# Edge-gated graph layer: load and rows steps of groups 2 and 3, and the lists of blocks 4 to 7 in shorter pieces

## The chip, the cores and the metric

The kernel runs on one core of one Trainium2 chip. Its time is the device time of one execution in microseconds. The kernel before was timed in nine runs: median 1203.03 us, lowest 1196.97, highest 1206.84.

## The reference

There are 16 batches of 1024 nodes with 256 features, and one adjacency matrix of 1024 x 1024 in which few entries are not zero (the diagonal and about 0.8% of the rest). Every edge (u, v) of every batch has a gate, a sigmoid of a small network on the two nodes. Gated and ungated sums over the edges go through one weight matrix each and are added to the input:

```python
pre_u = jnp.einsum('bud,dk->buk', h_t, W1[:d])
pre_v = jnp.einsum('bvd,dk->bvk', h_t, W1[d:])
hidden = jax.nn.relu(pre_u[:, :, None, :] + pre_v[:, None, :, :] + b1)
S = jax.nn.sigmoid(jnp.einsum('buvk,ko->buvo', hidden, W2)[..., 0] + b2[0])
a_t = jnp.einsum('buv,bud->bvd', S * A_a, h_t)
m_t = jnp.einsum('uv,bud->bvd', A_m, h_t) * h_t
z_t = beta1 * h_t + beta2 * (a_t @ Wa + ba) + beta3 * (m_t @ Wm + bm)
```

The last line is shortened here; both products there are einsums. `A_a` and `A_m` are the same matrix.

## The kernel before, in words

The 16 batches are four groups of four (g = 0 to 3). The 1024 target nodes v are eight tiles of 128 (vt = 0 to 7). A block is one (g, vt): 32 blocks, in the order of line 365: the first six tiles of groups 0 and 1, then tiles 6 and 7 of both, then groups 2 and 3. A block has ten steps, two windows of 64 target nodes with five slots of 128 edges each. Step n is block n // 10 and place s = n % 10, and there are 320 steps.

**Edges instead of the full matrix.** `lists(vt)` (line 236) finds the edges of a tile. It loads a tile of the adjacency matrix (`key`), finds the largest keys of every row (`max`), spreads them over slots, and leaves index tables: `uidx` (which node row to fetch), `vidx` (which matrix entry), `onehot`, `whose` and `rest` (what did not fit). It is a generator: each `yield` ends a piece, and each `next(made[vt])` runs one. Nearly all of its work is on DVE; the matmuls into `pw` and `pe` are small, and for vt >= 3 they use the PSUM buffers "misc", of which there are two and which `rows`, `halves`, `turn_over` and `block_end` use too. The lists of tiles 0 to 3 are made ahead of step 0. Those of tiles 4 to 7 are made inside the steps, where `advance` (line 659) says which step runs a piece.

**Tables.** A group's table holds, for every node, its product with the first half of W1 and its input, so that one gather fetches both. `load_hT(k)` loads a transposed tile of the input on SP's queue, and waits until one of the ten buffers "hT" is free. `copy_h(k)` copies the input tile into the table, from memory to memory, on ACT's queue. `rows(k)` makes the product in two pieces, each with eight matmuls for `w_u` (line 384) and a copy on ACT (line 400), and stores it one step after the second (line 403, SP's queue). For the tiles that are not made ahead of step 0, `plan` (line 665) gives a triple: the step of the load, and the steps of the two pieces. The four blocks in `again` have their hT loaded a second time.

**A step.** `expand(n + 2)` puts the target nodes' products into PSUM `pc` with two matmuls (line 523). `gate(n)` adds the fetched rows (DVE, line 539), takes the weighted sum of the positive part for four batches (DVE, line 543), then ACT takes the sigmoid (line 546) and scales the left factors (line 549). `aggregate(n - 1)` sums on PE with 8 or 16 matmuls (line 560). `fetch(n + 4)` gathers 128 table rows into one of five buffers "fetched" on POOL (line 453); it needs aggregate(n - 1) to have left that buffer, and the gathers of a group need its whole table. `fetch_val(2)` (line 341) issues up to two small gathers of matrix entries on POOL in each step, as long as any list has left some.

**Once a block.** `halves(k + 1)` multiplies the next block's hT by `w_v` at places 0 and 2 (line 384 again), and ACT copies at places 3, 5 and 6. `turn_over` transposes sums at places 1, 7 (twice) and 9. `block_end` multiplies by Wm and Wa at places 3 to 6. The output is stored at place 9 (line 615), and the input block is loaded at place 0 (line 714), both on SP's queue. A hT buffer becomes free when `times_h` (line 591, DVE) has read it, at place 3 of the block after the one that used it.

**Order.** The order of instructions on each engine and queue is written by hand: the loop of line 684 goes through the steps, and each engine works through its own in that order, waiting on semaphores only. SP has little but transfers, so it runs ahead of the steps until a transfer has to wait for data or for a buffer. What `after(step, f)` registers runs at `do(n)`, after gate(n). At step 100, POOL reduces `rest` over the partitions (line 761).

Of the kernel before, what the change touches and what calls it, by code (L numbers as in the profile page):

```python
# [11 lines left out]
ALU = mybir.AluOpType  # L12
AX = mybir.AxisListType
P = 128
# [3 lines left out]
def kernel(  # L18
# [42 lines left out]
    nc = tc.nc  # L61
    B, N, D = x.shape
    NT = N // P
# [41 lines left out]
    def fixed(shape, name, dt=FP):  # L105
        return const.tile(shape, dt, name=name)
# [5 lines left out]
    ukey = fixed([P, N], "ukey")  # L112
# [117 lines left out]
    EARLY = 4  # L230
# [3 lines left out]


    def lists(vt):
        key = fetched[vt + 1][:, :N] if vt < EARLY else big.tile([P, N], FP, name="key", bufs=1)
        (nc.sync if 2 <= vt < EARLY else nc.gpsimd).dma_start(key, adjT[vt * P:(vt + 1) * P, :])
        yield
# [1 line left out]
        top = R[:, 5:5 + S]  # L241
        count = wk.tile([P, 1], FP, name="count", bufs=4)
        unread = one.tile([P, N], mybir.dt.uint8, name="unread")
        nc.vector.scalar_tensor_tensor(key, key, 0.0, ukey, ALU.not_equal, ALU.mult)
        nc.scalar.activation(unread, key, AF.Sign, accum_out=count)
        yield

# [1 line left out]
        cand = wk.tile([P, N // P, 8], FP, name="cand", bufs=2)  # L249
        for c in range(N // P):  # L250
            nc.vector.max(cand[:, c, :], key[:, c * P:(c + 1) * P])
        yield
        cut = wk.tile([P, 1], FP, name="cut", bufs=2)
        nc.vector.tensor_reduce(cut, cand[:, :, 7], AX.X, ALU.max)
# [2 lines left out]
        for s in range(0, S, 8):  # L257
            nc.vector.max(top[:, s:s + 8], keys)
            if s + 8 < S:
                nc.vector.scalar_tensor_tensor(keys, keys, top[:, s + 7:s + 8], keys, ALU.is_lt, ALU.mult)  # L260

        used = wk.tile([P, S], FP, name="used", bufs=4)
        nc.vector.tensor_scalar(used, top, 0.0, None, ALU.is_gt, ALU.add, accum_out=R[:, 0:1])
# [29 lines left out]
        last = wk.tile([P, 1], FP, name="last", bufs=4)  # L293
        nc.vector.scalar_tensor_tensor(used, nth, held, top, ALU.is_equal, ALU.mult, accum_out=last)
        nc.vector.tensor_tensor(thr[:, vt:vt + 1], last, none, ALU.add)
        RR = wk.tile([P, NW, RC], FP, name="RR", bufs=2)
        few = wk.tile([P, E], mybir.dt.uint8, name="few", bufs=2)
        nc.scalar.copy(few, mark)  # L298
        for w, mine in enumerate((soon, late)):
            nc.vector.tensor_scalar(RR[:, w, :], R, mine, None, ALU.mult)  # L300
        yield
# [4 lines left out]
        for j in range(TW):  # L306
            nc.tensor.matmul(pe[:, j * NW * RC:(j + 1) * NW * RC], mark[:, j * P:(j + 1) * P],
                             RR.rearrange("p w r -> p (w r)"), start=True, stop=True)
        M = NW * TW
# [6 lines left out]
        eq = wk.tile([P, M, S], FP, name="eq", bufs=1)  # L316
        nc.vector.tensor_tensor(eq, nth.unsqueeze(1).to_broadcast([P, M, S]),
                                s_of.unsqueeze(2).to_broadcast([P, M, S]), ALU.is_equal)
        nc.vector.tensor_tensor(eq, eq, L[:, :, 5:], ALU.mult)
        k_of = wk.tile([P, M], FP, name="k_of", bufs=2)  # L320
        nc.vector.tensor_reduce(k_of, eq, AX.X, ALU.add)
        sl = slice(vt * NW, (vt + 1) * NW)
        nc.vector.tensor_scalar(uidx[:, sl].rearrange("p w j -> p (w j)"), k_of, -1.0, float(N), ALU.mult, ALU.add)
        nc.vector.tensor_tensor(k_of, L[:, :, 2], k_of, ALU.subtract)
# [132 lines left out]


    made = [lists(vt) for vt in range(NT)]
    turn = [(g, vt) for g in range(2) for vt in (*range(FIRST, NT), *range(FIRST))]  # L460
    tabs = [fetched[0][:, :GD], *(f[:, GD:] for f in fetched)]
# [195 lines left out]


    advance = {0: (3,), 2: (3,), 4: (3,)}
    for i, n in zip(range(EARLY, NT), (0, 20, 50, 80)):  # L660
        for o in (0, 4, 5, 6, 7, 9, 11, 13, 15, 17):
            advance[n + o] = (*advance.get(n + o, ()), i)
    loads, at = {}, {}

    def plan(blocks, ns):

        for k, (load, *pieces) in zip(blocks, ns):
            loads[load] = k
            at.update((n, k) for n in pieces)

    plan(turn[NT:], ((0, 5, 8), (6, 12, 15), (12, 18, 22), (17, 25, 28), (24, 32, 35), (31, 38, 42), (38, 45, 48),
                     (43, 50, 52)))
    plan([(2, vt) for vt in range(NT)], ((62 + 10 * i, 68 + 10 * i, 73 + 10 * i) for i in range(NT)))
    plan([(3, vt) for vt in range(NT)], ((146, 152, 157), (156, 162, 167), *((153 + 10 * i, 158 + 10 * i, 161 + 10 * i)
                                                                             for i in range(2, NT))))
    plan(again, ((103,), (113,), (125,), (133,)))
    begun = set(turn[:NT])
    end = parts = piece = last = None
# [5 lines left out]
    for n in range(total + 2):  # L684
        k, s = divmod(n, T)
# [25 lines left out]
        if s == 0 and 0 < k < BS:  # L711
            hbs[k - 1] = big.tile([P, GB, D], FP, name="h_blk", bufs=1)
            g, vt = order[k - 1]
# [56 lines left out]
    with tc.If(any_left > 0):  # L770
        with ExitStack() as s2:
# [3 lines left out]
            for vt in range(NT):  # L775
# [12 lines left out]
                key = fb.tile([P, N], FP, name="fb_key")  # L788
# [88 lines left out]
```

## Time and profile before

| | us |
|---|---|
| median of nine runs | 1203.03 |
| the profiled execution | 1199.47 |
| its span | 1197.7 |
| start of step 0 (first L539) | 74.0 |
| start of step 100 | 464.6 |
| start of step 160 | 665.2 |
| start of step 240 | 929.0 |

| engine | busy us | share of the span |
|---|---|---|
| PE, matmuls | 1101.6 | 92% |
| DVE | 1064.6 | 89% |
| ACT | 896.9 | 75% |
| POOL | 433.8 | 36% |

The DMA engines move 391 MB, 327 GB/s over the span. The busy time of PE is modelled where matmuls are pipelined, so 92% is no measure of how much it could still do. A step is found in the trace by its L539, the first DVE instruction of gate(n), of which there are 320. Times in the trace count from the start of the span.

### The profile page before, as it was taken

The page shows a single profiled execution, that of the slowest core. Times are in us where ns is not written, and L with a number is a line of the kernel's source. Part 1 is how long each engine was busy: PE and PEld are TensorE (multiplying, and loading weights), DVE is VectorE, ACT ScalarE, POOL GpSimd, SP SyncE. Part 2 cuts the span into 40 slices and gives each one's busy share as a digit, 9 for nine tenths or more (in the row PEclk, how much of TensorE's full clock was granted, in tenths as well). Part 3 has the DMA queues.
Part 4 walks back from the last instruction along what each step waited for, and adds up shares of the span by engine and source line. Part 5 has one row for each costly group of instructions (what it writes and reads, how often), then busy time and mean ns, then how long its engine had stood idle before and what let it go on. Part 6 is the DMA issues. An engine that isn't in the chain of part 4 may idle for free. (4 is left out here: it accounts for less than half of the span.)

```text
span 1197.7 us, 23914 instructions
## 1 busy us (share of the span) xinstructions
PE 1101.6 (92%) x7633; PEld 726.8 (61%) x7633; DVE 1064.6 (89%) x3483; ACT 896.9 (75%) x2624; POOL 433.8 (36%) x428
## 2 busy tenths in 40 slices
PE   6856899989899989999999999999999999999986
PEld 5743566656556656666666566666666666666653
DVE  7688879978998897999999889989999999999994
ACT  2346577768768867888888788888888888888873
POOL 1556762533253326333333233233323333333330
PEclk9878998989899999999999999999999999999999
DMA  9986898999988989999999999999999999999992
GB/s 280 284 281 232 263 342 319 347 327 339 336 281 301 380 281 312 368 376 378 384 349 359 336 338 361 347 367 367 361 359 361 348 323 331 322 337 329 333 348 84
DMA packets 147047, 391.40 MB, mean 327 GB/s; under 512 B 16752, under 2 KB 105328, under 8 KB 110704
## 3 DMA queue, kind: packets, MB, share of 16 engines
q0 software_dynamic: 50016, 300.50, 68.4%
q1 hardware_dynamic: 81616, 74.99, 19.7%
q10 hardware_dynamic: 15280, 14.29, 3.7%
q8 instruction: 63, 1.03, 0.3%
q14 instruction: 72, 0.59, 0.1%
HBM read 393.78 MB, written 50.33 MB: 371 GB/s over the span
## 5 line engine op out<-in xcount | busy, mean ns | idle before, releaser
L453 POOL DMA_INDIRECT fetched<-table,uidx x320 | 336.2, 1051 | 669.2 <-PE acc L560 514.5
L543 DVE SCALAR_TENSOR_TENSOR t<-t,w_b 128x256 f32<-128x256 f32 x1280 | 469.5, 422 | 22.0
L539 DVE TENSOR_TENSOR t<-fetched,pc 128x1024 f32<-128x1024 f32 x320 | 389.5, 1217 | 68.1 <-DMA fetched<-table,uidx 29.4
L560 PE MATMUL acc<-fetched,left 128*32 128x256 f32 x4096 | 342.0, 393 | 35.2 <-ACT left L549 29.3
L549 ACT ACTIVATE left<-left,gt 128x32 f32<-128x32 f32 (+1 forms) x1280 | 299.3, 304 | 10.4
L523 PE MATMUL pc<-X,mark 128*128 128x512 f32 x640 | 237.0, 452 | 12.3 <-DVE t L539 6.9
L560 PEld LDWEIGHTS acc<-fetched,left 128*32 128x32 f32 x4096 | 132.5, 110 | 185.6 <-ACT left L549 57.7
L523 PEld LDWEIGHTS pc<-X,mark 128*128 128x128 f32 x640 | 96.8, 190 | 147.2 <-issue 80.6
L546 ACT ACTIVATE gt<-sc,b_b 128x4 f32<-128x4 f32 x320 | 96.0, 300 | 56.1 <-DVE t L543 51.3
L384 PE MATMUL misc<-w_u,hT 128*128 128x256 f32 x448 | 110.9, 395 | 10.3 <-ACT few L298 3.6
L609 PE MATMUL misc<-w_m,LT 128*128 128x256 f32 x496 | 117.1, 379 | 0.0
L609 PE MATMUL misc<-w_a,LT 128*128 128x256 f32 x496 | 117.1, 379 | 0.0
L533 ACT ACTIVATE left<-onehot,val 128x128 f32<-128x128 bf16 (+1 forms) x320 | 116.5, 364 | 0.0
L384 PE MATMUL misc<-w_v,hT 128*128 128x256 f32 x448 | 106.6, 381 | 0.0
L543 DVE DVE_READ_ACCUMULATOR t<-t,w_b 128x1 f32 x1280 | 104.2, 81 | 0.0
L609 PEld LDWEIGHTS misc<-w_m,LT 128*128 128x128 f32 x496 | 94.0, 189 | 15.1
L609 PEld LDWEIGHTS misc<-w_a,LT 128*128 128x128 f32 x496 | 93.9, 189 | 14.9
L384 PEld LDWEIGHTS misc<-w_u,hT 128*128 128x128 f32 x448 | 87.1, 198 | 25.5 <-ACT few L298 3.7
L341 POOL DMA_INDIRECT val<-in_adjT_dram,vidx x80 | 84.7, 1059 | 31.3 <-issue 21.6
L384 PEld LDWEIGHTS misc<-w_v,hT 128*128 128x128 f32 x448 | 85.6, 191 | 13.9
L581 ACT COPY LT<-misc 128x512 f32<-128x512 f32 x128 | 70.9, 574 | 28.8 <-PE pc L523 10.2
L568 ACT COPY ev<-acc 128x512 f32<-128x512 f32 x128 | 75.5, 590 | 18.6 <-remote 7.1
(160 smaller groups left out, 898.7 us busy)
## 6 DMA issues: line engine op xcount, KB each, us to landing
h_blk<-in_x_dram SPq DMA_DIRECT2D x31, 512.0 KB
out_dram<-z SPq DMA_DIRECT2D x31, 512.0 KB
hT<-in_xT_dram SPq DMA_DIRECT2D x28, 512.0 KB
table<-tab SPq DMA_DIRECT2D x26, 512.0 KB
table<-in_x_dram ACTq DMA_DIRECT2D x24, 512.0 KB
fetched<-table,uidx POOLq DMA_INDIRECT x320
table<-in_x_dram SPq DMA_DIRECT2D x8, 512.0 KB
table<-fetched SPq DMA_DIRECT2D x6, 512.0 KB
```

The lines of the kernel that those rows point to most:

```text
L341: nc.gpsimd.indirect_dma_start(out=val[:, i, j:j + 1], out_offset=None, in_=adj_flat, in_offset=bass.IndirectOffsetOnAxis(ap=vidx[:, i, j: ...
L384: nc.tensor.matmul(p[:, bb * D:(bb + 1) * D], hT[:, 2 * h + bb, i, :], wt[:, i, :], start=(i == 0 and not begun), stop=(i == DC - 1), skip ...
L453: nc.gpsimd.indirect_dma_start(out=fetched[n % NF], out_offset=None, in_=table[g], in_offset=bass.IndirectOffsetOnAxis(ap=uidx[:, vt * NW ...
L523: nc.tensor.matmul(pcs[n][:, c], marks[n // TW][:, j * P:(j + 1) * P], cuts[k][:, w, c], start=True, stop=True)
L533: nc.scalar.activation(lefts[n][:, :m, :, 0, :], onehot[:, i, o:o + m, :].unsqueeze(2).to_broadcast([P, m, GB, V]), AF.Copy, scale=val[:, ...
L539: nc.vector.tensor_tensor(t, fetched[n % NF][:, :GD].rearrange("p (b d) -> p b d", b=GB), pcs.pop(n).rearrange("p (b d) -> p b d", b=GB), ...
L543: nc.vector.scalar_tensor_tensor(t[:, b, :], t[:, b, :], 0.0, w2_b, ALU.max, ALU.mult, accum_out=sc[:, b:b + 1])
L546: nc.scalar.activation(gt, sc, AF.Sigmoid, bias=b2_b)
L549: nc.scalar.activation(lefts[n][:, :m, b, 1, :], lefts[n][:, :m, b, 0, :], AF.Copy, scale=gt[:, b:b + 1])
L560: nc.tensor.matmul(accs[h][b * 2 * V:(b + 1) * 2 * V, r, :], left[:, i, b].rearrange("p k v -> p (k v)"), f[:, GD + b * D:GD + (b + 1) * D ...
L568: nc.scalar.copy(evs[q], accs.pop(q))
L609: nc.tensor.matmul(pz[:, bb * D:(bb + 1) * D], LTs[k][:, c, 2 * h + bb, i, :], wt[:, c, :], start=False, stop=(i == 0 and c == DC - 1), sk ...
```

## The change

Two things are changed. In `lists`, for tiles 4 to 7 alone (`fine`), six more yields are put in, and the first multiplication is done in two halves; `advance` runs a piece at offset 0 and then one in every step from offset 4 on, from the start steps 0, 19, 48 and 88 instead of 0, 20, 50 and 80. A list has 16 pieces, so the call at offset 19 finds nothing left.

In the plan for groups 2 and 3 other steps are given. Group 2: loads at 60 + 10i (before 62 + 10i), pieces at 68 + 10i and 71 + 10i (before 68 + 10i and 73 + 10i). Group 3: the loads of tiles 0 and 1 at 141 and 149 (before 146 and 156), those of tiles 2 to 7 at 153 + 10i as before; pieces of tiles 0 and 1 at 149, 151 and 158, 161 (before 152, 157 and 162, 167), of tiles 2 to 6 at 161 + 10i and 168 + 10i (before 158 + 10i and 161 + 10i), and of tile 7 at 231 and 234 (before 228 and 231).

```diff
     def lists(vt):
+        fine = vt >= EARLY
         key = fetched[vt + 1][:, :N] if vt < EARLY else big.tile([P, N], FP, name="key", bufs=1)
...
-        nc.vector.scalar_tensor_tensor(key, key, 0.0, ukey, ALU.not_equal, ALU.mult)
+        if fine:
+            nc.vector.scalar_tensor_tensor(key[:, :N // 2], key[:, :N // 2], 0.0, ukey[:, :N // 2],
+                                           ALU.not_equal, ALU.mult)
+            yield
+        rest_ = slice(N // 2 if fine else 0, N)
+        nc.vector.scalar_tensor_tensor(key[:, rest_], key[:, rest_], 0.0, ukey[:, rest_], ALU.not_equal, ALU.mult)
         nc.scalar.activation(unread, key, AF.Sign, accum_out=count)
         yield
...
             nc.vector.max(cand[:, c, :], key[:, c * P:(c + 1) * P])
+            if fine and c == N // P // 2 - 1:
+                yield
...
                 nc.vector.scalar_tensor_tensor(keys, keys, top[:, s + 7:s + 8], keys, ALU.is_lt, ALU.mult)
+            if fine and s == 8:
+                yield
...
         nc.vector.tensor_tensor(thr[:, vt:vt + 1], last, none, ALU.add)
+        if fine:
+            yield
...
                                 s_of.unsqueeze(2).to_broadcast([P, M, S]), ALU.is_equal)
+        if fine:
+            yield
         nc.vector.tensor_tensor(eq, eq, L[:, :, 5:], ALU.mult)
         k_of = wk.tile([P, M], FP, name="k_of", bufs=2)
         nc.vector.tensor_reduce(k_of, eq, AX.X, ALU.add)
+        if fine:
+            yield
...
-    for i, n in zip(range(EARLY, NT), (0, 20, 50, 80)):
-        for o in (0, 4, 5, 6, 7, 9, 11, 13, 15, 17):
+    for i, n in zip(range(EARLY, NT), (0, 19, 48, 88)):
+        for o in (0, *range(4, 20)):
             advance[n + o] = (*advance.get(n + o, ()), i)
...
-    plan([(2, vt) for vt in range(NT)], ((62 + 10 * i, 68 + 10 * i, 73 + 10 * i) for i in range(NT)))
-    plan([(3, vt) for vt in range(NT)], ((146, 152, 157), (156, 162, 167), *((153 + 10 * i, 158 + 10 * i, 161 + 10 * i)
-                                                                             for i in range(2, NT))))
+    plan([(2, vt) for vt in range(NT)], ((60 + 10 * i, 68 + 10 * i, 71 + 10 * i) for i in range(NT)))
+    plan([(3, vt) for vt in range(NT)], ((141, 149, 151), (149, 158, 161), *((153 + 10 * i, 161 + 10 * i, 168 + 10 * i)
+                                                                             for i in range(2, NT - 1)), (223, 231, 234)))
```

## The prediction, made before the changed kernel was seen

> **What bounds the kernel now.** I read the page first, then the windows view with an edge at the first L539 of every tenth step (a step is one gate(n); ten steps are one block), then the waits, then the timeline wherever a block was longer than its neighbours.
>
> The windows view, one row a block:
>
> ```profile
> core 0: us, PE busy (x) PEld busy (x) DVE busy (x) ACT busy (x) POOL busy (x), PEclk, DMA share, GB/s
> 388.30:428.80 40.50, 36.93 (x264) 24.01 (x262) 36.35 (x126) 30.63 (x91) 11.24 (x12) 0.96 0.95 344
> 428.80:464.60 35.80, 33.90 (x238) 22.73 (x242) 34.61 (x116) 27.58 (x81) 15.60 (x15) 1.00 0.84 291
> 464.60:501.20 36.60, 34.93 (x244) 22.90 (x236) 30.19 (x95) 27.89 (x83) 15.90 (x17) 1.00 1.01 361
> 501.20:534.10 32.90, 32.71 (x240) 21.65 (x232) 30.44 (x99) 27.81 (x82) 10.15 (x10) 1.00 1.02 376
> 632.10:665.20 33.10, 31.69 (x219) 20.79 (x216) 30.29 (x97) 26.52 (x77) 9.78 (x10) 1.00 0.97 352
> 665.20:700.90 35.70, 33.09 (x232) 21.58 (x232) 30.27 (x96) 27.52 (x83) 10.09 (x11) 1.00 0.89 325
> 700.90:734.30 33.40, 33.13 (x242) 21.36 (x243) 30.25 (x95) 28.09 (x87) 11.83 (x12) 1.00 1.00 361
> 734.30:765.60 31.30, 29.56 (x210) 19.47 (x209) 30.15 (x97) 26.24 (x79) 10.18 (x10) 1.00 0.99 357
> 929.00:960.30 31.30, 30.15 (x218) 19.22 (x217) 30.15 (x96) 26.33 (x80) 10.53 (x11) 1.00 0.96 350
> ```
>
> These are blocks 8 to 11, 15 to 18 and 24. Block 24 has only gates and aggregates: 31.3 us, of which DVE works 30.2. That is the floor, and block after block from 24 to 30 takes it. Block 18 has two pieces of rows as well and still takes 31.3. Blocks 8 and 9 share the list of block 7, which adds (36.35 + 34.61) - 2 x 30.2 = 10.6 us of DVE work; there DVE is the bound. In block 11 the DMA share is 1.02 and PE is busy nearly throughout. Blocks 15, 16 and 17 have no list, and stand 1.8, 4.4 and 2.1 us above the floor.
>
> The waits, and the timeline at the worst place of block 16:
>
> ```profile
> POOL fetched L453 <- PE acc L560: 514.5, 229, 6.9
> ...
> DVE t L539 <- DMA fetched<-table,uidx: 29.4, 27, 3.7
> ```
>
> ```profile
> 674.50 1.22 DVE L539 TENSOR_TENSOR t<-fetched,pc 128x1024 f32<-128x1024 f32 x1 [3.69 <-DMA fetched<-table,uidx]
> ...
> 676.58 1.89 PE L384 MATMUL misc<-w_v,hT 128*128 128x256 f32 x8
> ...
> 678.30 1.89 PE L384 MATMUL misc<-w_u,hT 128*128 128x256 f32 x8
> ...
> 681.49 0.99 POOL L453 DMA_INDIRECT fetched<-table,uidx  x1 [5.55 <-PE acc L560]
> ```
>
> The reader is to see a ring: PE aggregates, that frees a fetched buffer, POOL issues the gather, DVE gates, ACT makes left, PE aggregates. A late PE makes the next gather late, and a gather that is late is what DVE waits for. In block 16 the products for w_v (halves) and w_u (rows, step 162) fall on one step, and just before it three 512 KB transfers leave SP together: the timeline has table<-tab at 664.13, out at 664.57, h_blk at 665.34.
>
> **What the Trainium skill says.** "Perfetto Trace Analysis", Optimization Strategy: the most-contended engine can change between regimes, and interleaving regimes can help. The trace agrees: DVE bounds the list blocks (DMA 0.84 in block 9), DMA and PE the next ones. "DMA: Bandwidth & Descriptors", Issuing engines are not separate DMA queues: transfers of SP, ACT and POOL run on the same 16 engines. The trace agrees with shares of 1.00 to 1.02, so moving a transfer moves a delay. "TensorE: Matmul & The Clock Gate", Part 1, says that an idle PE falls to half clock; the page's PEclk has digits of 7 and 8 in early slices, and I price nothing by it.
>
> **The change, part by part.** The profiled execution took 1199.47 us (span 1197.7), the median of the nine runs is 1203.03; I sum against the former and move the median by the same amount.
>
> 1. Rows at the start of group 3. Pieces move from steps 152, 157, 162, 167, 178 to 149, 151, 158, 161, and one goes to the end (234). From i = 2 on, the other pieces keep the same steps (181, 188, ... 231) with another half in each. A piece is 8 matmuls, 1.89 us by the timeline row. Block 16 loses one of its two pieces and the collision at its third step, block 17 loses its only one, and block 15's go to its second and ninth steps, where PE has only an aggregate, an expand and at most a transpose. Before, the three blocks take 33.1 + 35.7 + 33.4 = 102.2 us. Blocks 20 to 23, with pieces at just these places, take 31.7, 32.5, 32.9 and 32.0 in the same view, a mean excess of 1.0 over the floor. With 3 x 32.3 = 96.9 the gain is 5.3 us. At most it is 102.2 - 93.9 = 8.3; at least 0, if DMA and not PE holds these blocks. I take 5.3.
>
> 2. Rows of group 2. The second pieces go from the fourth step of a block (73 + 10i) to its second (71 + 10i). The fourth already has 16 aggregating matmuls and the first products of block_end. In block 7 this ends a wait of 2.01 us at L539 of step 76 for PE pc; I count 1.0 back, and 0.3 in block 14. Blocks 6, 8, 9 are held by DVE, blocks 10 to 13 by DMA (shares 1.00 to 1.02): nothing there. The loads go from 62 + 10i to 60 + 10i. On SP this moves nothing: SP runs ahead, and hT (L373) already leaves about 0.6 us after h_blk (349.69, then 350.28), so "two steps earlier" is true of copy_h on ACT's queue only. Its 512 KB take about 512/370 = 1.4 us of the DMA engines, now beside out, h_blk and hT. In list blocks DVE hides it. In blocks 10 to 13 gathers for the fourth step are late already (up to 2.98 us), but PE is busy through those waits; bounds 0 to 4 x 1.4, taken 1.3. The table store comes two steps earlier, far from its first gather. Sum of the part 0.0.
>
> 3. The lists. The work on DVE stays: one multiplication of 1.22 us becomes two of half, some 0.1 us each list more, 0.4 in all. Within steps 24 to 39, 54 to 69 and 84 to 99 DVE idles no more than in the clean blocks, so an even spread gains nothing there. List 7 moves: its pieces run in steps 92 to 106, not 84 to 97. In block 10 the same view has DVE at 30.19 of 36.60 us, so 5.3 us of stall (floor idle taken off) in which list work could lie; four of the fifteen pieces, 10.6 x 4/15 = 2.8 us, fall on its steps 102 to 106. POOL's ten fetches of val (about 1.06 us each, two a step, between gathers) leave steps 96 to 100 for 106 to 110, so their delay of the gathers moves with them. I take -2.0 for list 7; bounds -5 and +3. List 4: pw's misc buffer is held for one step, not two, and the wait of 2.08 us on PE misc at step 8 may go: -0.3. The rest of list 7 is read by partition_all_reduce (L761) one step after it is made, not eleven; POOL starts that only after the gather of the same step, 0.21 us later at 475.20, by when DVE has done it: nothing. Sum -1.9.
>
> 4. The end of group 3. Step 234 gets a piece in the fifth step of block 23, which has little room (PE 31.4 of 32.0): +0.7. Behind it the store of the last half leaves at 235 instead of 232 in program order. On the chip the store of a piece leaves some 2.1 steps after it (905.83 for step 231, where step 233 begins at 906.3), so near 916.6. By the packets of the trace such a store moves most of its bytes 2 to 6 us after issue and the last by about 9, so it lands at 923 to 926. The gather for step 240, the first to read this table, was issued at 919.67:
>
> ```profile
> 916.48 0.99 POOL L453 DMA_INDIRECT fetched<-table,uidx  x1 [2.05 <-PE acc L560]
> 919.67 0.99 POOL L453 DMA_INDIRECT fetched<-table,uidx  x1 [2.20 <-PE acc L560]
> 922.98 0.99 POOL L453 DMA_INDIRECT fetched<-table,uidx  x1 [2.32 <-PE acc L560]
> 926.06 0.99 POOL L453 DMA_INDIRECT fetched<-table,uidx  x1 [2.09 <-DVE z L613]
> ```
>
> This is the timeline of POOL. It will wait 4 to 6 us, and all gathers behind it on POOL with it. The gather's packets end about 2 us after POOL's 0.99, near 922.6, and DVE wants it at 929.0: a cover of 6.4 us, less what out and h_blk take just then. Bounds 0 and +4; taken +1.4. Sum +2.1.
>
> Together -5.3 + 0.0 - 1.9 + 2.1 = -5.1 us: 1194.4 for an execution like the profiled one, 1197.9 for the median.
>
> **The rivals.** *No change*: blocks 15 to 17 are held by DMA, the same bytes have to pass, and the gain of part 1 is given back in blocks 18 to 23; only -2 of part 1 is left, part 3 gains nothing. For it: shares of 0.97 and 1.00 in blocks 15 and 17. Against it: 0.89 in the worst, block 16, and block 18 at the floor with 0.99. -2 + 0 + 0.4 + 2.1 = about +0.5, 1203.5.
> *Slower*: the burst. copy_h now follows h_blk and hT at once in eight blocks (6 to 13); if gathers of the fourth and fifth steps really wait for it, each block loses up to 1.4 us, 11 in all; and the end costs 4 + 0.7. For it: the late gathers at the fourth step (0.5 to 3.0 us in blocks 10 to 13). Against it: PE has no idle time in those waits, and the list blocks hide it. It decides from about 0.9 us a block on, where 8 x 0.9 eats parts 1 and 3. Price: 11 + 4.7 - 5.3 - 1.9 = +8.5, 1211.5.
> *The lists matter more*: if spreading them also ends the early half-clock stretches and the stalls of blocks 0 to 4 (blocks 0 to 2 and 4 stand several us above their DVE work), 8 us more go: 1190.
>
> **How the numbers follow.** A measurement here tells about 0.3%, 3.6 us, from no change. The main case, 1197.9, has 0.42, and is split by its spread of about 4 us: 0.29 faster, 0.10 within, 0.03 slower. The larger gain has 0.16, all faster. No change has 0.19: 0.03 faster, 0.13 within, 0.03 slower. The burst has 0.23: 0.04 within, 0.19 slower. Sums: faster 0.48, within 0.27, slower 0.25. The main case alone would span 1192 to 1203; with both far ends the range is 1188 to 1210.
>
> **What would show it.** Right: block 16 near 32 us with no wait of over 1 us on a gather, block 17 near 31.6; POOL waiting for table<-tab about 5 us once before step 240, with DVE losing under 2; block 8 at about 35. Wrong: blocks 16 and 17 still above 33; waits on gathers at the fourth or fifth steps of blocks 6 to 13 longer than now; new stalls in blocks 10 and 11 where list 7 and its val fetches now lie.

## The result, and the profile after

The changed kernel took 1188.63 us in the median of 10 runs (1185.25 to 1193.25), beside 1203.03 us before: a ratio of 0.9885, 95% interval 0.9862 to 0.9908, or -14.4 us where -5.1 was predicted. Timed again later, beside three other kernels, the ratio was 0.9941 (0.9915 to 0.9968), 1190.63 beside 1199.19 us. The ratios are over fast runs alone (those within 1.5% of the fastest of their kernel), and are not quite the quotients of the medians beside them. The two intervals just miss each other: the two estimates of the gain are some 14 and 7 us, and the intervals together reach from about 4 to 17 us. The profiled execution shown below took 1191.13 us (span 1189.3), a second one 1187.41. Line numbers of the changed kernel are higher by 16 from the steps on: gate is L555 where it was L539, rows and halves L400 (L384), the gather L469 (L453).

The windows view of the changed kernel, for the same blocks as before (8 to 11, 15 to 17, 24; edges at the first L555 of every tenth step):

```profile
core 0: us, PE busy (x) PEld busy (x) DVE busy (x) ACT busy (x) POOL busy (x), PEclk, DMA share, GB/s
383.90:415.50 31.60, 31.60 (x232) 20.99 (x228) 30.05 (x96) 26.89 (x82) 10.59 (x11) 1.00 1.01 371
415.50:456.20 40.70, 37.12 (x270) 24.24 (x262) 36.45 (x128) 31.23 (x92) 11.47 (x12) 1.00 0.92 330
456.20:493.20 37.00, 32.24 (x213) 21.72 (x214) 34.49 (x115) 24.91 (x73) 16.01 (x16) 1.00 0.93 319
493.20:531.10 37.90, 34.99 (x229) 23.30 (x229) 30.71 (x99) 27.28 (x84) 15.39 (x15) 0.91 0.91 307
629.40:662.30 32.90, 32.90 (x236) 22.17 (x238) 30.17 (x97) 27.27 (x82) 10.10 (x10) 1.00 0.99 366
662.30:694.10 31.80, 31.24 (x232) 20.04 (x224) 30.26 (x97) 27.20 (x83) 10.03 (x10) 1.00 0.98 352
694.10:726.60 32.50, 31.05 (x223) 19.80 (x222) 30.17 (x97) 26.58 (x80) 11.49 (x11) 1.00 1.00 359
919.50:952.60 33.10, 32.30 (x237) 20.44 (x234) 30.31 (x97) 26.99 (x83) 12.28 (x11) 1.00 0.97 361
```

Block 16 falls from 35.7 to 31.8 us, block 17 from 33.4 to 32.5. Block 8 is free of its list and takes 31.6, not 40.5; but the work of the list (DVE 36.45 and 34.49 instead of 30.2) now lies in blocks 9 and 10, and block 11, with no list work left, takes 37.9 us where it took 32.9, with POOL busy for 15.4 us instead of 10.2. Block 24 is 1.8 us longer.

One trace is one execution, so I compare stretches over all traces taken. "Old" and "new" are the two forms of the part that acts in the stretch; all kernels are those of the experiments below, without the two that thin out the val gathers.

| steps | what differs | old, us (traces) | new, us (traces) |
|---|---|---|---|
| 0 to 100 | lists | 390.1 (7) | 387.2 (4) |
| 100 to 150 | lists | 168.3 (7) | 170.7 (4) |
| 150 to 180 | rows, tiles 0 and 1 of group 3 | 102.4 (4) | 96.5 (8) |
| 180 to 240 | rows, tiles 2 to 7 of group 3 | 196.6, from 192.2 to 201.5 (4) | 193.0, from 191.9 to 194.4 (8) |
| 240 to 260 | the end of rows | 63.1 (4) | 64.0 (8) |

The list rows leave out the kernel that has list 7 at 80. The sum is -9.0 us. The stretch before step 0, where nothing was changed, varies between 69.5 and 74.0 us from trace to trace, and 74.0 was that of the trace read for the prediction.

### The profile page after: what moved, and what is told of

The parts are those of the page before. It is cut to its first block, busy times and chain, and to the rows that moved or that the text cites. A ratio compares the mean times of both kernels' runs of the same rounds, so it can differ in the third digit from the quotient of the medians.

```text
span 1189.3 us, 23919 instructions
## 1 busy us (share of the span) xinstructions
PE 1096.4 (92%) x7633; PEld 726.3 (61%) x7633; DVE 1063.9 (89%) x3487; ACT 894.4 (75%) x2624; POOL 436.0 (37%) x428
## 5 line engine op out<-in xcount | busy, mean ns | idle before, releaser
L469 POOL DMA_INDIRECT fetched<-table,uidx x320 | 339.3, 1060 | 661.1 <-PE acc L576 529.7
L555 DVE TENSOR_TENSOR t<-fetched,pc 128x1024 f32<-128x1024 f32 x320 | 389.5, 1217 | 56.9 <-DMA fetched<-table,uidx 28.2
L539 PE MATMUL pc<-X,mark 128*128 128x512 f32 x640 | 237.7, 453 | 15.3 <-DVE t L555 10.3
L539 PEld LDWEIGHTS pc<-X,mark 128*128 128x128 f32 x640 | 97.1, 191 | 149.8 <-issue 78.0
L400 PE MATMUL misc<-w_u,hT 128*128 128x256 f32 x448 | 107.6, 386 | 6.0 <-ACT few L310 3.6
L400 PE MATMUL misc<-w_v,hT 128*128 128x256 f32 x448 | 107.5, 383 | 0.0
L400 PEld LDWEIGHTS misc<-w_u,hT 128*128 128x128 f32 x448 | 84.8, 194 | 18.0 <-ACT few L310 3.7
L400 PEld LDWEIGHTS misc<-w_v,hT 128*128 128x128 f32 x448 | 86.2, 192 | 14.0
```

What stands on the lines that cost most here:

```text
L400: nc.tensor.matmul(p[:, bb * D:(bb + 1) * D], hT[:, 2 * h + bb, i, :], wt[:, i, :], start=(i == 0 and not begun), stop=(i == DC - 1), skip ...
L469: nc.gpsimd.indirect_dma_start(out=fetched[n % NF], out_offset=None, in_=table[g], in_offset=bass.IndirectOffsetOnAxis(ap=uidx[:, vt * NW ...
L539: nc.tensor.matmul(pcs[n][:, c], marks[n // TW][:, j * P:(j + 1) * P], cuts[k][:, w, c], start=True, stop=True)
L555: nc.vector.tensor_tensor(t, fetched[n % NF][:, :GD].rearrange("p (b d) -> p b d", b=GB), pcs.pop(n).rearrange("p (b d) -> p b d", b=GB), ...
```

## The experiments

Each was timed in five rounds; ratios are against the kernel before on the same chip.

| kernel | median us | before us | ratio, 95% interval |
|---|---|---|---|
| new plan of groups 2 and 3, old lists | 1191.8 | 1200.18 | 0.9916, 0.9885 to 0.9947 |
| the same, later | 1191.55 | 1200.3 | 0.9919, 0.9887 to 0.9950 |
| new lists, old plan | 1201.67 | 1200.18 | 0.9994, 0.9965 to 1.0024 |
| group 3 alone | 1190.72 | 1200.18 | 0.9913, 0.9883 to 0.9943 |
| group 2 alone | 1199.25 | 1200.18 | 0.9996, 0.9974 to 1.0018 |
| group 3, tiles 0 and 1 alone | 1189.82 | 1199.19 | 0.9931, 0.9905 to 0.9957 |
| group 3, tiles 2 to 7 alone | 1194.88 | 1199.19 | 0.9970, 0.9942 to 0.9997 |
| changed kernel, again | 1190.63 | 1199.19 | 0.9941, 0.9915 to 0.9968 |
| changed, last pieces at 229 and 231 | 1190.64 | 1199.19 | 0.9938, 0.9913 to 0.9963 |
| changed, list 7 at 80 | 1189.02 | 1200.3 | 0.9883, 0.9825 to 0.9941 |
| changed, one val gather a step | 1163.6 | 1200.3 | 0.9672, 0.9625 to 0.9719 |
| new plan, old lists, one val gather a step | 1161.29 | 1200.3 | 0.9668, 0.9619 to 0.9716 |

**Which part carries it.** Four kernels, each the kernel before with some of the change. The plan:

```diff
-    plan([(2, vt) for vt in range(NT)], ((62 + 10 * i, 68 + 10 * i, 73 + 10 * i) for i in range(NT)))
-    plan([(3, vt) for vt in range(NT)], ((146, 152, 157), (156, 162, 167), *((153 + 10 * i, 158 + 10 * i, 161 + 10 * i)
-                                                                             for i in range(2, NT))))
+    plan([(2, vt) for vt in range(NT)], ((60 + 10 * i, 68 + 10 * i, 71 + 10 * i) for i in range(NT)))
+    plan([(3, vt) for vt in range(NT)], ((141, 149, 151), (149, 158, 161), *((153 + 10 * i, 161 + 10 * i, 168 + 10 * i)
+                                                                             for i in range(2, NT - 1)), (223, 231, 234)))
```

> The new plan of groups 2 and 3 with the lists as before (10 pieces, starts 0, 20, 50, 80). The change as a whole measured -14.4 us. My prediction's terms give -5.3 + 0.0 + 2.1 = -3.2 us for the plan, so about 1200; blocks 16 and 17 near 32 us. Rival 'the rows are worth more': -8 us or more (under 1195), and the lists add little. Rival 'the lists carry it': 0 to -4 us here.

The lists alone, which are the rest of the diff:

> The new lists (16 pieces, starts 0, 19, 48, 88) with the plan as before. My prediction's term is -1.9 us, about 1201. Rival 'the lists carry it': -8 us or more, under 1195, with DVE's waits in blocks 0 to 10 smaller. If both parts together give less than -14.4 us, they help each other (rows and list pieces collide on the same steps); if more, they overlap.

Group 3's two lines of the plan alone, and group 2's one line alone:

> Only group 3's plan is new. My terms 1 and 4: -5.3 + 2.1 = -3.2 us, about 1200. Blocks 15 to 17 near 97 us in sum (before 102.2). If the end costs nothing, -5 us. Rival 'DMA holds these blocks': within 1 us of before, because blocks 18 to 23 give it back.

> Only group 2's plan is new: loads two steps earlier, second pieces at the second step of a block, not the fourth. My term 2: 0 us, 1203. Rival 'the burst': +4 to +8 us from copy_h beside out, h_blk and hT in blocks 6 to 13. Rival 'the fourth step was overloaded': -3 to -6 us, with fewer waits of DVE for PE in blocks 7 and 10 to 14.

Group 3 alone has the whole gain of the plan (0.9913 beside 0.9916 and 0.9919). Group 2 alone and the lists alone make no difference that can be measured. So the rival of the burst falls: group 2's interval ends at 1.0018, +2 us, where the burst was priced at 11 us. Earlier copies and earlier second pieces were not run apart, so it is their sum that is shown to be nothing. The rival of the lists falls too.

**Two places in group 3.** The triples of tiles 0 and 1, and those of tiles 2 to 7, each alone:

```diff
-    plan([(3, vt) for vt in range(NT)], ((146, 152, 157), (156, 162, 167), *((153 + 10 * i, 158 + 10 * i, 161 + 10 * i)
+    plan([(3, vt) for vt in range(NT)], ((141, 149, 151), (149, 158, 161), *((153 + 10 * i, 158 + 10 * i, 161 + 10 * i)
```

> Only the triples of tiles 0 and 1 of group 3 are new (141, 149, 151 and 149, 158, 161); all else as before. Theory 'collision' (my term 1: two products of 1.9 us and three transfers met in block 16): blocks 15 and 16 fall to 65 us in sum from 68.7, and the time by -4 us or more. Theory 'late tile' (the tile of the input for rows lands only 7 to 21 us after its issue, PE needs it 18.7 us after, and PE waits): 0 to -2 us, as tiles 2 to 7 still have five steps between load and first piece.

```diff
-    plan([(3, vt) for vt in range(NT)], ((146, 152, 157), (156, 162, 167), *((153 + 10 * i, 158 + 10 * i, 161 + 10 * i)
-                                                                             for i in range(2, NT))))
+    plan([(3, vt) for vt in range(NT)], ((146, 152, 157), (156, 162, 167), *((153 + 10 * i, 161 + 10 * i, 168 + 10 * i)
+                                                                             for i in range(2, NT - 1)), (223, 231, 234)))
```

> Only the triples of tiles 2 to 7 of group 3 are new (pieces eight and fifteen steps after the load, not five and eight); tiles 0 and 1 as before. Theory 'late tile': -5 us or more, and no PE wait for DMA hT from block 18 on. Theory 'collision': 0 to -2 us (block 17 loses its one piece) and +1.4 at the end, so about 1200 where before has 1200.

Both gain, 0.9931 and 0.9970, the second by little (its interval ends at 0.9997). That the gains add is not shown by these times: the changed kernel, timed beside them, has 0.9941, no more than tiles 0 and 1 alone. The traces keep the two places apart.

With the new triples of tiles 0 and 1, blocks 15 to 17 take 96.6 us where these alone are new, and at most 97.4 in any of the eight that have them; with the old ones, at least 101.2. Step by step, this is not the collision of two products that I had priced. Steps 162 to 164, in which w_v and w_u meet, take 10.3 us in the mean with the old triples and 10.1 with the new; and in the trace of before, the wait of 3.69 us ends at 674.50, ahead of both products (676.58 and 678.30). The long steps are others:

| step | old, us (4 traces) | new, us (8 traces) |
|---|---|---|
| 159 | 4.3 to 4.9 | 3.2 to 3.3 |
| 161 | 4.3 to 6.5 | 2.9 to 3.8 |
| 169 | 3.8 to 4.1 | 3.2 to 3.3 |
| 171 | 4.0 to 4.5 | 2.9 to 3.7 |
| 172 | 3.7 to 3.8 | 2.9 |

They come in two like groups, behind the second pieces of tiles 0 and 1 (steps 157 and 167, place 7). In PE's order such a piece stands right behind two transposes of `turn_over` at the same place, and both use the two "misc" buffers. PE in the trace of before, then in that of the changed kernel, where the next piece of rows is at step 158:

```profile
659.17 1.03 PE L578 MATMUL misc<-ident,ev 128*128 128x128 f32 x8
661.49 1.99 PE L384 MATMUL misc<-w_u,hT 128*128 128x256 f32 x8 [1.28 <-ACT LT L581]
663.41 1.07 PE L560 MATMUL acc<-fetched,left 128*32 128x256 f32 x16
```

```profile
656.72 1.04 PE L594 MATMUL misc<-ident,ev 128*128 128x128 f32 x8
657.68 1.64 PE L576 MATMUL acc<-fetched,left 128*32 128x256 f32 x16
```

Before, PE waits 1.28 us until ACT has copied the transposed sums (`LT`) out, then makes the product, and the aggregate that the ring needs starts 3.2 us after the transposes have ended. In the changed kernel it follows them at once. All four old traces have this wait twice, for the pieces of steps 157 and 167, and none of the new ones has it. Behind such a piece, too, the store of its table, the output and the input block leave SP within 1.2 us in the trace of before (664.13, 664.57, 665.34, and again 699.81, 700.23, 700.67); in the changed kernel the two stores leave at steps 153 and 163, by themselves. So what is shown is the place of the second piece, with its store; how much of the 5.8 us comes from PE and how much from the three transfers together is not, as one triple moves both.

Steps 180 to 240 depend on the other triples. With the old ones, the tile of the input for rows (512 KB) leaves SP at place 4 of a block and PE wants it 16 to 19 us later; by the packets of the traces, it lands 7 to 23 us after its issue. In the kernel with tiles 0 and 1 alone it came late. Its traced execution, 1198.57 us, is one of the longest of that kernel (median 1189.82). The waits of that stretch (waiter, awaited: us in total, times, longest), then lines of its timeline, from 737 to 766 us:

```profile
DVE t L539 <- PE pc L523: 6.2, 1, 6.2
PE misc L384 <- DMA hT<-in_xT_dram: 6.1, 1, 6.1
```

```profile
737.89 0.37 SPq L373 DMA_DIRECT2D hT<-in_xT_dram  x1
...
760.99 3.75 PE L384 MATMUL misc<-w_u,hT 128*128 128x256 f32 x8 [6.12 <-DMA hT<-in_xT_dram]
```

The load leaves at 737.89, and PE sits at the piece for 6.12 us until it is there, 23 us after; half of its packets had ended within 4.6 us, and the last at 22.6. DVE then loses as much as PE. Block 19 took 39.9 us in this trace. The same eight matmuls usually take 1.89 us and here 3.75. The Trainium skill, "TensorE: Matmul & The Clock Gate", Part 1, says that an idle PE falls to half clock; this trace agrees, with a granted clock of 0.50 from 759 to 763 us. The trace read for the prediction already had the wait, and so had the kernel with the new lists alone:

```profile
PE misc L384 <- DMA hT<-in_xT_dram: 2.6, 3, 1.7
```

```profile
PE misc L400 <- DMA hT<-in_xT_dram: 4.0, 1, 4.0
```

These are the waits of the kernel before from 734 to 930 us, and of the lists alone from 733 to 932. In the changed kernel no PE wait for hT is left from 726 to 920 us: the first piece now comes 26 us after the load (738.6 to 764.9 for tile 3). Nor is there one in the other seven traces with the new triples. In the four old ones the stretch is the longer, the longer these waits are: 192.2 us without any, 194.7 with 2.6 us, 197.7 with 4.0, 201.5 with 6.1. So this part of the gain is there in some executions and not in others, and one trace of before showed little of it.

**The end of rows.** The last two pieces of group 3 two or three steps earlier:

```diff
-                                                                             for i in range(2, NT - 1)), (223, 231, 234)))
+                                                                             for i in range(2, NT - 1)), (223, 229, 231)))
```

> The changed kernel, but the last two pieces of group 3 run at 229 and 231, not 231 and 234. My term 4 says that the end costs 0.7 + 1.4 = 2.1 us: then -2 us against the changed kernel, and block 24 back at 31.3 us. If the wait of POOL for table<-tab is covered, the time stays within 0.5 us of the changed kernel.

> The changed kernel unaltered, for a second trace and for a time beside the three others on one chip. Between -10 and -17 us against before by the first comparison (ratio 0.9862 to 0.9908). If the lists and group 2 add to group 3's plan, it is 2 to 4 us below what group 3's plan alone gave (0.9913); if not, equal.

No difference (0.9938 beside 0.9941), and block 24 stays long, at 32.9 us. So the late last piece isn't what makes block 24 longer. The wait that I had priced does not occur: in the changed kernel's timeline of SP and POOL,

```profile
908.17 0.33 SPq L419 DMA_DIRECT2D table<-tab  x1
```

```profile
908.48 1.19 POOL L469 DMA_INDIRECT fetched<-table,uidx  x1 [3.63 <-PE acc L576]
911.87 1.09 POOL L469 DMA_INDIRECT fetched<-table,uidx  x1 [2.20 <-PE acc L576]
```

the store of the table leaves at 908.17, and the second of these gathers, for step 240, waits for PE and not for the table. By its packets the store was over 2.5 us after its issue, beside 36 packets of gathers (0.3 MB). The store of before at 905.83 had taken 9.5 us, beside 368 of them (3.0 MB). Block 24 is 0.9 us longer in the mean: DVE waits for gathers there, for 0.5 to 3.3 us in all, in seven of the eight new traces (1.7 in the changed kernel), and for 0, 0, 0.4 and 1.4 us in the old ones. What delays these gathers stays open.

**The lists, and what the val gathers do.** List 7 at its old start step, and the new plan with the old lists once more:

```diff
-    for i, n in zip(range(EARLY, NT), (0, 19, 48, 88)):
+    for i, n in zip(range(EARLY, NT), (0, 19, 48, 80)):
```

> The changed kernel with list 7 starting at 80, as before, not 88. My term 3 gave the later start -2.0 us, so +2 us against the changed kernel. Rival 'it only moves the stalls': within 1.5 us, with block 8 back at 38 to 40 us and blocks 9 and 11 shorter by as much.

> The new plan of groups 2 and 3 with the old lists once more, beside the three others. If the new lists add nothing, its ratio to before is that of the changed kernel (0.9885 and 0.9941 so far), about 0.9915; if they are worth 2 us or more as my term 3 says, it is 0.993 or above.

The start step makes no difference that these intervals can show (0.9883, 0.9825 to 0.9941). In the trace, block 8 is back at 39.2 us and block 11 at 31.6: the stall moves with the list. Block 8 is long mostly by the list's own work, as it still takes 37.9 us with the old lists and one val gather a step. The stall behind a list comes from the val gathers that follow it, as the last two kernels show. In each, one number is changed, in the changed kernel and in the new plan with the old lists:

```diff
-            fetch_val(2)
+            fetch_val(1)
```

> The changed kernel with one small gather of matrix entries a step (fetch_val) in place of two. In four traces with the new lists, blocks 10 to 14 take 2.6 us more than in six with the old ones, most of it in block 11, just after list 7's ten val gathers (steps 106 to 110). Theory 'POOL cannot keep up' (a gather and two val gathers need 3.9 us of POOL, a step has 3.1): block 11 falls by 3 us or more, also waits in blocks 1, 2, 4 and 7, -4 to -8 us against the changed kernel. Rival 'PE and DMA hold them': within 2 us of it.

> The new plan with the old lists, and one val gather a step. If POOL's val gathers cause the stalls of blocks 4, 7 and 10, -4 us or more against the new plan alone; if this is also below the changed kernel with one val gather, the new lists are worth nothing.

Both take some 37 to 39 us less than the kernel before, and some 25 to 30 less than their own forms with two val gathers. All of that lies ahead of step 150 (557 and 560 us in the two traces of the changed kernel, 530 with one val gather a step; from there to step 320, 559 to 560 in all three), and the number of val gathers is 80 in both. That is several times what I had expected. The windows view of blocks 7 and 11, first of the changed kernel, then with one val gather a step:

```profile
345.50:383.90 38.40, 33.22 (x227) 22.00 (x227) 30.52 (x97) 26.88 (x81) 15.32 (x15) 0.96 0.92 313
493.20:531.10 37.90, 34.99 (x229) 23.30 (x229) 30.71 (x99) 27.28 (x84) 15.39 (x15) 0.91 0.91 307
```

```profile
334.70:366.40 31.70, 31.70 (x230) 20.87 (x227) 30.25 (x97) 27.19 (x82) 16.17 (x16) 1.00 1.00 366
473.10:505.80 32.70, 32.61 (x231) 21.27 (x230) 30.56 (x99) 27.31 (x82) 16.51 (x17) 1.00 1.04 384
```

DVE does the same work in both (30.5 and 30.3 us in block 7), but its idle time goes from 7.9 to 1.4 us. Block 7 even has one more of POOL's instructions (16, not 15), and still is 6.7 us shorter: what matters is that they don't come in a clump. The timeline of POOL in the changed kernel shows the clump, and below it the same place with one val gather a step:

```profile
484.54 1.00 POOL L357 DMA_INDIRECT val<-in_adjT_dram,vidx  x1 [0.30 <-issue]
485.84 1.08 POOL L357 DMA_INDIRECT val<-in_adjT_dram,vidx  x1 [0.30 <-issue]
487.23 0.99 POOL L469 DMA_INDIRECT fetched<-table,uidx  x1 [0.31 <-issue]
488.53 1.00 POOL L357 DMA_INDIRECT val<-in_adjT_dram,vidx  x1 [0.30 <-issue]
489.83 1.04 POOL L357 DMA_INDIRECT val<-in_adjT_dram,vidx  x1 [0.30 <-issue]
492.22 0.99 POOL L469 DMA_INDIRECT fetched<-table,uidx  x1 [1.34 <-PE misc L400]
```

```profile
469.19 0.99 POOL L469 DMA_INDIRECT fetched<-table,uidx  x1 [1.30 <-PE acc L576]
470.48 1.00 POOL L357 DMA_INDIRECT val<-in_adjT_dram,vidx  x1 [0.30 <-issue]
472.62 1.47 POOL L469 DMA_INDIRECT fetched<-table,uidx  x1 [1.13 <-PE acc L576]
```

With two, POOL takes one instruction after the other with 0.3 us between, about 3.9 us a step where a step of the list-free blocks takes 3.1, so the gathers fall behind the ring. With one, POOL waits for PE again, as it does in the rest of the kernel. The place is shown; whether POOL's own time or the small packets of these gathers on the DMA engines weigh more is not, since both are halved together. With one val gather a step the two forms of the lists take the same time (1163.6 and 1161.29 us, ratios 0.9672 and 0.9668). These two are the fastest kernels here, and the intervals don't part them.

## Why the prediction was right, and where its sum was off

The direction and the main place were right; the sum was too small, and the mechanism named for its largest term was not the one that acts. That 1188.6 lies inside the range, at its edge, owes something to luck: the range went below 1192 only for the rival of the lists, and that rival fell. By the second ratio, 0.9941 of 1203.03, the time is about 1196, which is within the main case.

*Part 1, rows at the start of group 3.* Predicted 102.2 to 96.9 us for blocks 15 to 17; over the traces 102.4 to 96.5. The comparison with blocks that have pieces at the same places gave the sum, though the cause named with it was not the one at work; so far the closeness is luck. Of the 5.8 us, steps 162 to 164, with the products for w_v and w_u, have 0.2. Nor does block 17 gain by losing its piece at step 178: with tiles 0 and 1 alone it keeps that piece and takes 31.7 us, and with tiles 2 to 7 alone it loses it and takes 33.9. The second pieces at place 7, and the stores behind them, are what the new triples of tiles 0 and 1 change.

What failed in the sum is the sentence after it, "From i = 2 on, the other pieces keep the same steps (181, 188, ... 231) with another half in each", to which I gave no cost at all. The steps of the products stay, but the distance from load to first piece grows from five steps to eight, and that removes a PE wait: -3.6 us in the mean of the traces (196.6 to 193.0, from four traces and eight). The wait stood in the waits of the profile before, at 2.6 us. This missing term is the step that failed. The timed kernels alone would not establish its size: tiles 2 to 7 alone gain 0.3%, with an interval that just leaves out none.

*Part 2, group 2.* Predicted 0.0; measured 0.9996 (0.9974 to 1.0018). Right in sum; its terms of about 1 us are too small to be checked.

*Part 3, the lists.* Predicted -1.9; measured 0.9994 alone, and no gain in the company of the plan. The hiding of list work in block 10 did happen: it takes 37.0 us with 34.49 of DVE work, and took 36.6 with 30.19. That is 4.3 us of list work, not 2.8, as seven of the fifteen pieces fall on its steps (100 to 106) and I had counted four; steps 0 to 100 are 2.9 us shorter. The sentence "their delay of the gathers moves with them" was right as well, but I did not charge it: the ten val gathers now leave in steps 106 to 111, and steps 100 to 150 are 2.4 us longer.

*Part 4, the end.* Predicted +2.1; traces +0.9, of which no part is a wait for the table. The landing time of a store was carried over from a place with more gathers beside it.

*The rivals.* No change: falls. The burst: falls with group 2 alone. "The lists matter more" came near in its price, 1190, but was wrong as put: the new lists alone gain nothing (0.9994). One val gather a step does shorten blocks 0 to 4, to 187 us from at least 200 in the traces with two. Of the signs named, block 16 near 32 came (31.8); block 8 fell further than said (31.6, not 35); the wait for the table did not come; and one sign of being wrong, a new stall in block 11, did.

Of the traced -9.0 us, group 3's two places make -9.4, the lists -0.5 and the end +0.9. The timed gain of 7 to 14 us is compatible with that; where within it the true value lies is open.

## What to carry to other kernels

For every step that is moved, count the distance from its load as well as the engine that it lands on: a transfer that lands anywhere between 7 and 23 us after its issue needs a lead of its longest, not of its median. When work of a second kind shares an in-order queue with the transfers that feed a ring, compare the queue's time for a step with the step itself; here a few instructions that together last longer than the step (3.9 us against 3.1) stalled all engines, though the queue was idle on average (POOL was busy for 36% of the span). And take a wait that shows small in one trace as a sample: it may be 1.7 us in one execution and 6 in the next.

## What was not expected of the hardware

A 512 KB load of the transposed input took 7 to 23 us to land in the same kernel and at the same place of a block, while a 512 KB store took 2.5 us with 0.3 MB of gathers beside it and 9.5 us with 3.0 MB. The Trainium skill, "DMA: Bandwidth & Descriptors", Issuing engines are not separate DMA queues, says that all transfers interleave on the same engines; the two stores agree with that, and what spread the loads was not taken apart. And a PE that had waited 6.1 us for such a load ran its next eight matmuls in 3.75 us, not 1.89, so that the wait cost more than its length.
